# Two attention blocks on one core: the small matrix G transposed by a DMA on halves of its words instead of by TensorE, in six of eight images

## The chip, the cores and the metric

The kernel runs on one core of a Trainium2 chip. The metric is the device time of one launch, in microseconds (us). The core has five instruction streams that run beside each other and meet only at semaphores: TensorE (PE; its weight loads are listed as PEld), VectorE (DVE), ScalarE (ACT), GpSimd (POOL) and SyncE (SP), which here only issues DMAs. Each stream takes its instructions in the order written, so an instruction that waits holds up everything behind it on its stream, the DMA queue of SyncE included.

## The reference

The input x has 8 images of 512 channels and 64 x 64 pixels. Two layers follow each other.

```python
# layer 0
f = conv1x1(x, Wf, bf)                                  # 64 channels, 4096 pixels
g = maxpool2x2(conv1x1(x, Wg, bg)); v = maxpool2x2(conv1x1(x, Wh, bh))
beta = softmax(einsum('bcn,bcm->bnm', f, g), axis=-1)
o = einsum('bcm,bnm->bcn', v, beta)
x = gamma * conv1x1(o, Wv, bv) + x
# layer 1
Q = wq x + bq; K = wk x + bk; V = wv x + bv
Qf = delu(Q).transpose(0, 2, 1); Kf = delu(K)           # delu(x) = 10 relu(x) + exp(10 min(x, 0))
KV = einsum('bmn,bcn->bmc', Kf, V)
norm = 1 / einsum('bnd,bd->bn', Qf, sum(Kf, -1) + EPS)
out = x + gamma * einsum('bnd,bdc,bn->bcn', Qf, KV, norm)
```

All is in 32-bit floats. Layer 1 is linear in V, so the kernel does not form V. It sums G = Kf x^T (64 x 512) over an image and then multiplies by wv once: KV = G wv^T plus a term of the bias. That product needs G with its 512 channels on the partitions, hence a transposed G.

## The kernel before

An image is cut into 8 chunks of 512 pixels, 64 chunks in all. The program is a loop over steps s; one step works on several chunks at different stages at once. Layer 0's exponentials E of chunk s+1 are made and summed while the products M of chunk s (values by normalised E, in seven block products after Winograd and Strassen) and its projection N back to 512 channels run. The last chunk's layer 1 features are used in the same step, and f, g and v of chunk a = s + 9 are formed. Each piece is registered with a number, `at(t, fn)`, and the pieces of a step are issued in the order of t. So t is a place in an order written by hand, not a time, and it holds on all five streams.

The first step of an image (j == 0) closes the image before it, b_c. Step 8 is the first such step. These pieces of it matter, with t and line:

- `gather(s-1)` at 12.6 and 13.5: the last product pg (L727) and its addition to G (L736, VectorE). G is a tile of 128 x 512: rows 0 to 63 hold the sum of even blocks of pixels, rows 64 to 127 that of odd ones.
- `normalize` at 12.65, 13.7 and 38.6: the divisors pd of layer 1 (L818), their reciprocal rq_pd on VectorE (L825), its way to DRAM (L827, tile rn_row) and back, spread over the partitions (L831, two DMAs, tile rn), and at 38.6 the product qq (L837). The reciprocal lies in a tile of tag "rq", which has one buffer.
- `total` and `invert` of chunk s+1 at 17.85 and 18.0: the sum of E over the keys (L464) and its reciprocal on VectorE (L474), into a tile of the same tag "rq".
- `spread_inverses` at 18.01: this reciprocal to DRAM (L479, tile rd) and back on all partitions (L481, tile rb). `keep_inverses` at 23.0: ScalarE copies it to PSUM (L485, tile rtot). `normalize_block` multiplies the quarters of E by it (L499, VectorE, from 24.3 on).
- `bias_v` at 18.5, `split_v` at 18.6 and `turn_v` at 18.7: bias and transposition of v (L359 and L366 on ScalarE, L371 on SyncE); `join_v` at 32.0.
- `turn_G` at 21.2: four matmuls with the matrix `two` (L774), whose product is the transposed G with its two halves of rows added, and a copy scaled by gamma to the tile gT (L778, ScalarE).
- `project` at 24.8 and after: N in seven products; the first is copied out by ScalarE (L596, twice for one pair of blocks), added to x by GpSimd (L599), and its bank is then used on by the fourth product. Further additions are on VectorE (L602, L607).
- `features` at 35.0 (L633), and `features_exp` and so on.
- `make_KV` in the next step, at 5.5: pkv from gT and the weights (L791), after the first three M products and before the exponentials' products s (L407) of that step.

Words are transposed elsewhere in the kernel by a DMA that can turn 16-bit elements: ScalarE splits 32-bit words into high and low halves (`split_x` L682, 128 x 1024 halves), SyncE issues a transposing DMA (`turn_halves` L688), and a copy joins the halves (`join_x` L695 on ScalarE, `join_k` L674 on GpSimd with half as many). Chunks of x use the tiles w0 to w3 and u0 to u3 for that, one buffer each; the splits of a step stand at 33.8 to 36.8.

Scratch tiles come from a pool of seven buffers of 128 x 512 words, in turn; PSUM's eight banks are given out in turn as well.

Of the kernel before, what the change touches and what calls it, by code (L numbers as in the profile page):

```python
# [36 lines left out]
F32 = mybir.dt.float32  # L37
U16 = mybir.dt.uint16
AF = mybir.ActivationFunctionType
ALU = mybir.AluOpType  # L40
# [4 lines left out]
P = 128  # L45
QP = 32
CH = 512
# [4 lines left out]
def tile_two_attention_blocks(  # L52
# [21 lines left out]
    nc = tc.nc  # L74
    B, C, H, W = x.shape
    N = H * W
    D = WfT.shape[1]
    CV = WhT.shape[1]
    KT = C // P
# [5 lines left out]
    TOTAL = B * NCHUNK  # L85
# [24 lines left out]
    g1 = const.tile([P, 1], F32, name="g1")  # L110
# [69 lines left out]
    def run(ctx, general):  # L180
# [6 lines left out]
        work1 = ctx.enter_context(tc.tile_pool(name="work1", bufs=1))  # L187
# [7 lines left out]
        def bank(name):  # L195
            return psum.tile([P, CH], F32, tag="m", name=name)

        def scratch(name):
            return temp.tile([P, CH], F32, tag="t", name=name)
# [39 lines left out]
        st = {}  # L239
# [479 lines left out]
        def gather(s, at, t, t_out):  # L719

            b, j = divmod(s, NCHUNK)
            G, m = st[b]["G"], {}

            def product():
                pg = m["pg"] = bank(f"pg_{s}")
                for t in range(NT):
                    nc.tensor.matmul(  # L727
                        pg[half(t % 2), :], kTs[s][:, t, :], xTs[s][:, t, :],
                        start=(t < 2), stop=(t >= NT - 2),
                    )  # L730

            def out():
                if j == 0:
                    nc.vector.tensor_copy(G, m["pg"])
                else:
                    nc.vector.tensor_tensor(G, G, m["pg"], ALU.add)  # L736

            at(t, product)
            at(t_out, out)
# [24 lines left out]
                    kb[half(e), half(e)], ones[half(e), 0:D], ksum[half(e)], EPS, ALU.mult, ALU.add  # L764
                )

        def turn_G(b, at, t):

            s = st[b]

            def product():
                pt = bank(f"pGT_{b}").rearrange("p (k d) -> p k d", d=P)[:, :, 0:D]
                for k in range(KT):
                    nc.tensor.matmul(  # L774
                        pt[:, k, :], s["G"][:, bass.ts(k, P)], two, start=True, stop=True
                    )
                gT = s["gT"] = work1.tile([P, KT, D], F32, tag="gT", name=f"gT_{b}")
                nc.scalar.mul(gT, pt, g1)  # L778

            at(t, product)  # L780

        def make_KV(b, at, t, t_out):

            s = st[b]
            hc = C // 2

            def product():
                pkv = s["pkv"] = bank(f"pkv_{b}")
                for k in range(KT):
                    for h in range(2):  # L790
                        nc.tensor.matmul(  # L791
                            pkv[half(h), 0:hc], s["gT"][:, k, :], s["w_v1"][:, k, bass.ts(h, hc)],
                            start=(k == 0), stop=(k == KT - 1),
                        )

            def out():
                kv = s["kv"] = work1.tile([P, C], F32, tag="kv", name=f"kv_{b}")
                for h in range(2):
                    c = bass.ts(h, hc)
                    nc.vector.scalar_tensor_tensor(  # L800
                        kv[half(h), c], b_v1[half(h), c], s["ksum"][half(h)], s["pkv"][half(h), 0:hc],
                        ALU.mult, ALU.add,
                    )
                nc.gpsimd.tensor_copy(kv[half(1), 0:hc], kv[half(0), 0:hc])
                nc.vector.tensor_copy(kv[half(0), hc:C], kv[half(1), hc:C])

            at(t, product)
            at(t_out, out)
# [147 lines left out]
        def step(s):  # L956
            here, after = 0 <= s < TOTAL, 0 <= s + 1 < TOTAL
            a = s + LEAD
            b, j = divmod(s, NCHUNK)
            b_c = b - 1  # L960
# [4 lines left out]
            def at(t, fn, *args):  # L965
                work.append((t, len(work), fn, args))
# [45 lines left out]
                    gather(s - 1, at, *((30.9, 32.6) if late_k else (12.6, 13.5)))  # L1012
            if c_here and here and j == 0:
                at(0.2, start_kb, b_c)
                turn_G(b_c, at, 21.2 if a < TOTAL else 19.5)
                if a >= TOTAL:
                    make_KV(b_c, at, 21.4, 24.2)
            if s == TOTAL - NCHUNK:
# [32 lines left out]
            if after:  # L1051
                n = s + 1
# [6 lines left out]
                if not here:  # L1059
                    t, t_invert = 24.85, 24.86  # L1060
                elif s == 0 or a == TOTAL:
                    t, t_invert = 21.2, 22.6
                elif a > TOTAL and s % 2 == 0:
                    t, t_invert = 19.55, 19.6
                else:
                    t, t_invert = 16.1 if j % 2 == 1 and c_here else 17.85, 18.0
# [47 lines left out]
            if s == TOTAL:  # L1114
                pairs = [first // 2 + i for i in range(NCHUNK // 2)]
                x_last[s - 1] = [x_b[s - 1][:, k, :] for k in range(KT)]
                stored[s - 1] = [(x_b[s - 1], 0, KT)]
                at(-0.45, copy_x, s - 1)
                at(0.1, turn_k, s - 1)
                at(0.2, start_kb, B - 1)  # L1120
                gather(s - 1, at, 0.25, 0.35)
                at(0.4, divisors, pairs[0])
                turn_G(B - 1, at, 0.5)
                at(0.6, divisors, pairs[1])
                at(0.7, invert_divisors, 0)
                make_KV(B - 1, at, 0.9, 1.2)
                at(1.0, spread, pairs[0])
                at(1.1, divisors, pairs[2])
                at(1.15, spread, pairs[1])
                at(1.25, divisors, pairs[3])  # L1130
                at(1.3, scale, pairs[0])
                at(1.4, scale, pairs[1])
                at(1.6, invert_divisors, 1)
                for i, p in enumerate(pairs):
                    for k in range(KT):
                        at(7.0 + 4 * i + k, finish_last, p, k)
                    if i < 2:
                        at(8.6 + i, spread, pairs[i + 2])
                        at(10.5 + i, scale, pairs[i + 2])
                    for h in range(2):  # L1140
                        at(8.5 + 4 * i + 2 * h, store_last, p, h)
# [6 lines left out]
        for s in range(-LEAD, TOTAL + 1):  # L1148
            step(s)
# [5 lines left out]
    with ExitStack() as stack, tc.manual_schedule(engines=ENGINES):  # L1155
        run(stack, general=False)
# [12 lines left out]
    with tc.If(again > 0):  # L1169
        with ExitStack() as stack, tc.manual_schedule(engines=ENGINES):  # L1170
            run(stack, general=True)
# [37 lines left out]
```

## Time and profile before

| | us |
|---|---|
| median of 3 runs | 2599.88 (2599.7 to 2600.54) |
| the profiled execution | 2600.86 |
| its span, first to last instruction | 2599.0 |
| TensorE busy | 2561.7 |
| VectorE busy | 1957.4 |
| ScalarE busy | 1587.6 |
| GpSimd busy | 772.0 |

The profile is of one execution. A group of its page is one line of the kernel with one form of instruction: busy time in all, mean length in ns, idle time of the engine just before them and what ended most of it. The chain of waits follows the end of the program back from instruction to what released it. The timeline lists instructions in order of time, in us from the start of the span. A 32-bit matmul is recorded as two passes, each with its weight load. For a DMA the record is that of its issue on the queue.

### The profile page before, as it was taken

Reading aid. Unit: us, or ns where it says so; the run is one execution under the profiler, and the core shown is the slowest. Engines: PE = TensorE matmul, PEld = TensorE weight load, DVE = VectorE, ACT = ScalarE, POOL = GpSimd, SP = SyncE. Lnnn points to the kernel's source line nnn. Section 1 sums busy time; section 2 is a strip of 40 time slices with the busy share of each in tenths; the row PEclk is TensorE's granted clock in tenths of the full one; section 3 lists DMA queues with packets and bytes.
Section 4 is the critical chain, followed back from the end, with each engine's and each line's share of the span. In section 5 each row is a group of like instructions: output and inputs, shape, how many; then the busy total and the mean of one; then the engine's idle time right before and its main releaser. Section 6 shows DMA issues by size and latency. Waiting matters only on the chain.

```text
span 2599.0 us, 32002 instructions
## 1 busy us (share of the span) xinstructions
PE 2561.7 (99%) x11207; PEld 1765.2 (68%) x11207; DVE 1957.4 (75%) x3000; ACT 1587.6 (61%) x2724; POOL 772.0 (30%) x618
## 2 busy tenths in 40 slices
PE   8999999999999999999999999999999999999997
PEld 6667767667667667676676676666676666766664
DVE  5777778777777777777777777777777777788884
ACT  3375566566665675665665665666755656656662
POOL 4422323322323324223233223332233232221112
PEclk9999999999999999999999999999999999999999
DMA  5154455576565675565755566755657655665658
GB/s 171 55 136 100 130 146 141 135 177 138 148 168 132 167 175 123 160 158 135 178 143 156 150 137 161 188 130 148 164 131 183 142 149 146 146 144 141 160 142 278
DMA packets 488730, 390.68 MB, mean 150 GB/s; under 512 B 342072, under 2 KB 357360, under 8 KB 488560
## 3 DMA queue, kind: packets, MB, share of 16 engines
q1 hardware_dynamic: 471312, 329.03, 46.1%
q0 software_dynamic: 15232, 58.72, 12.3%
q8 instruction: 91, 1.49, 0.2%
q10 hardware_dynamic: 2016, 0.79, 0.1%
q14 instruction: 79, 0.65, 0.1%
HBM read 173.41 MB, written 133.39 MB: 118 GB/s over the span
## 4 chain that ended last, share of the span: by engine, by line
PE 90%; DVE 3%; DMA 1%; issue 1%; ACT 0%; POOL 0%; DVEq 0%; ACTq 0%; SPq 0%
PE M L523 29%; PE N L586 14%; PE H L316 12%; PE s L407 8%; PE pk L633 8%; PE fg L272 7%; PE pg L727 4%; PE pa L855 4%; PE tot L464 1%; PE pa L934 1%; DVE E L499 1%; PE pkv L791 1%; DMA xb<-in_x_dram 0%; PE pd L818 0%; DMA rb<-rd 0%
## 5 line engine op out<-in xcount | busy, mean ns | idle before, releaser
L599 POOL TENSOR_TENSOR xb<-xb,n 128x512 f32<-128x512 f32 x192 | 245.2, 1277 | 470.7 <-ACT n L596 460.2
L523 PE MATMUL M<-T,S 128*128 128x256 f32 x1536 | 364.5, 388 | 0.0
L499 DVE TENSOR_TENSOR E<-E,rtot 128x1024 f32<-128x1024 f32 x256 | 307.4, 1223 | 70.8 <-ACT rtot L485 68.9
L523 PEld LDWEIGHTS M<-T,S 128*128 128x128 f32 x1536 | 282.8, 190 | 81.1 <-ACT E L411 24.9
L695 ACT COPY xT<-u 128x1024 uint16<-128x1024 uint16 x252 | 328.3, 1353 | 1.4
L682 ACT COPY w<-xb 128x1024 uint16<-128x1024 uint16 x252 | 244.8, 1042 | 88.0 <-DVE xb L602 88.0
L596 ACT ACTIVATE n<-N,gb_v 128x256 f32<-128x256 f32 x384 | 161.1, 471 | 215.3 <-PE N L586 215.3
L411 ACT ACTIVATE E<-s 128x512 f32<-128x512 f32 x512 | 256.9, 619 | 33.4 <-DVE T L514 18.9
L674 POOL COPY kT<-uk 128x512 uint16<-128x512 uint16 x56 | 67.1, 1198 | 621.3 <-DMA uk<-wk 621.3
L586 PE MATMUL N<-to,w_v 128*128 128x256 f32 x1024 | 243.8, 380 | 3.8 <-ACT n L596 3.6
L407 PE MATMUL s<-f,g 64*128 64x512 f32 x1024 | 240.0, 604 | 2.8 <-DVE o L532 2.8
L523 PE MATMUL M<-E,vT 128*128 128x256 f32 x1024 | 231.8, 379 | 2.1 <-DVE E L499 2.1
L633 PE MATMUL pk<-xb,w_kqk 128*128 128x512 f32 x512 | 230.5, 593 | 1.9 <-DVE xb L607 1.9
L305 POOL TENSOR_TENSOR tha<-xa 128x512 f32<-128x512 f32 x59 | 80.6, 1366 | 499.1 <-PE M L523 462.2
L586 PEld LDWEIGHTS N<-to,w_v 128*128 128x128 f32 x1024 | 193.2, 190 | 33.9 <-ACT n L596 6.9
L602 DVE TENSOR_TENSOR xb<-xb,N 128x512 f32<-128x512 f32 x256 | 173.6, 683 | 55.5 <-POOL xb L599 53.3
L523 PEld LDWEIGHTS M<-E,vT 128*128 128x128 f32 x1024 | 194.4, 190 | 29.7 <-issue 3.4
L272 PE MATMUL fg<-xa,w_fg 128*128 128x512 f32 x472 | 212.5, 593 | 0.0
L445 DVE TENSOR_TENSOR r<-E 128x1024 f32<-128x1024 f32 x64 | 78.4, 1225 | 166.5 <-ACT E L411 166.5
L586 PE MATMUL N<-o,w_v 128*128 128x256 f32 x768 | 188.4, 381 | 1.7 <-ACT n L596 0.9
L586 PEld LDWEIGHTS N<-o,w_v 128*128 128x128 f32 x768 | 144.6, 190 | 56.5 <-issue 35.7
L485 ACT COPY rtot<-rb 128x512 f32<-128x512 f32 x54 | 31.8, 589 | 240.9 <-DMA rb<-rd 240.9
(160 smaller groups left out, 4516.1 us busy)
## 6 DMA issues: line engine op xcount, KB each, us to landing
xb<-in_x_dram SPq DMA_DIRECT2D x64, 1024.0 KB
out_dram<-xb SPq DMA_DIRECT2D x63, 1024.0 KB
xa<-in_x_dram SPq DMA_DIRECT2D x59, 1024.0 KB
out_dram<-y POOLq DMA_DIRECT2D x56, 1024.0 KB, 10.6
rb<-rd SPq DMA_DIRECT2D x54, 256.0 KB
w_v<-in_L_conv_wv_dram SPq DMA_DIRECT2D x8, 1024.0 KB
rn<-rn_row SPq DMA_DIRECT2D x56, 128.0 KB
x_early<-in_x_dram SPq DMA_DIRECT2D x4, 1024.0 KB
```

Of the source, the lines that this page charges most:

```text
L272: nc.tensor.matmul(fg, w_fg[:, k, :], x_a[a][:, k, :], start=(k == 0), stop=(k == KT - 1))
L316: nc.tensor.matmul(m[i], w_h7[i][:, k, :], th[a][i][:, k, :], start=(k == 0), stop=(k == hk - 1))
L407: nc.tensor.matmul(sc[e], g[half(e), i, :], fs[s][half(e), :], start=True, stop=True)
L411: nc.scalar.activation(es[s][:, 2 * i + e, :], sc[e], AF.Exp)
L499: nc.vector.tensor_tensor(b, b, r, ALU.mult)
L523: nc.tensor.matmul(m[i], v7[i][:, k, :], te[s][i][:, k, :], start=(k == 0), stop=(k == hm - 1))
L586: nc.tensor.matmul(a[:, k, :], w_v7[i][:, bass.ts(k, P)], b, start=not more and k == 0, stop=True, skip_group_check=more or k > 0,)
L599: nc.gpsimd.tensor_tensor(of_x(*ij), of_x(*ij), u, ALU.add)
L602: nc.vector.tensor_tensor(of_x(*ij), of_x(*ij), m[i], op)
L633: nc.tensor.matmul(pk, w_kqk[:, i, e * D : (e + 2) * D], x_b[s][:, i, :], start=(i == 0), stop=(i == KT - 1),)
L682: nc.scalar.copy(w, x_b[s][:, k, :].bitcast(U16).rearrange("p (n h) -> p h n", h=2))
L695: nc.scalar.copy(v[:, k], u)
```

## The change

In the six images that are closed while a chunk is still being prepared (`a < TOTAL`, steps 8, 16, 24, 32, 40 and 48), G is split into high and low halves by ScalarE (128 x 1024 halves), turned by a DMA from SyncE, joined by GpSimd into a scratch tile g2, and VectorE adds its two halves and scales the sum by gamma. The four stand at 13.6, 13.65, 22.5 and 38.7 of the same step. The old form, under the name `turn_G_now`, stays in the last two images.

```diff
-        def turn_G(b, at, t):
+        def turn_G_now(b, at, t):
...
+        def turn_G(b, at, ts):
+
+            s = st[b]
+            w = work1.tile([P, 2, CH], U16, tag="w3", name=f"wG_{b}")
+            u = work1.tile([P, 2 * KT, P], U16, tag="u3", name=f"uG_{b}")
+            g2 = scratch(f"g2_{b}").rearrange("p (k i) -> p k i", k=KT)
+
+            def split():
+                nc.scalar.copy(w, s["G"].bitcast(U16).rearrange("p (n h) -> p h n", h=2))
+
+            def turn():
+                nc.sync.dma_start_transpose(out=u, in_=w.rearrange("p h n -> p (h n)"))
+
+            def join():
+                nc.gpsimd.tensor_copy(
+                    g2.bitcast(U16).rearrange("p k (i h) -> p h k i", h=2),
+                    u.rearrange("p (h k) i -> p h k i", h=2),
+                )
+
+            def out():
+                gT = s["gT"] = work1.tile([P, KT, D], F32, tag="gT", name=f"gT_{b}")
+                nc.vector.scalar_tensor_tensor(
+                    gT, g2[:, :, 0:D], 1.0, g2[:, :, D:P], ALU.mult, ALU.add
+                )
+                nc.vector.tensor_scalar(gT, gT, g1, None, ALU.mult)
+
+            for t, fn in zip(ts, (split, turn, join, out)):
+                at(t, fn)
...
-                turn_G(b_c, at, 21.2 if a < TOTAL else 19.5)
+                if a < TOTAL:
+                    turn_G(b_c, at, (13.6, 13.65, 22.5, 38.7))
+                else:
+                    turn_G_now(b_c, at, 19.5)
...
-                turn_G(B - 1, at, 0.5)
+                turn_G_now(B - 1, at, 0.5)
```

## The prediction

> **What bounds the kernel now.** I read the page first, then the chain of waits, then the timeline of one affected step, then the waits. On the page TensorE is busy nearly all the time and the chain that ended last is 90% TensorE:
>
> ```profile
> PE 2561.7 (99%) x11207; PEld 1765.2 (68%) x11207; DVE 1957.4 (75%) x3000; ACT 1587.6 (61%) x2724; POOL 772.0 (30%) x618
> PE 90%; DVE 3%; DMA 1%; issue 1%; ACT 0%; POOL 0%; DVEq 0%; ACTq 0%; SPq 0%
> ```
>
> So work taken off TensorE could pay. The chain of waits prices the removed work, in step 8 (first image turned):
>
> ```profile
> 421.04 3.65 PE M L523 x16
> 424.69 0.84 PE pGT L774 x8
> 425.53 3.49 PE fg L272 x8
> 429.02 4.57 PE N L586 x20
> ```
>
> pGT holds the chain for 0.84 us; the change drops it for six images, 6 x 0.84 = 5.0 us at most. But twenty passes of N at 0.214 us are 4.28, and the chain gives 4.57: 0.29 us of waiting is inside. The timeline of the same step (start, length, engine, line; in brackets the idle time before and its releaser) says for what:
>
> ```profile
> 419.60 0.68 DVE L736 TENSOR_TENSOR G<-G,pg 128x512 f32<-128x512 f32 x1
> 420.19 0.95 DVE L825 RECIPROCAL rq_pd<-pd 128x128 f32<-128x128 f32 x1
> 421.17 0.60 SPq L827 DMA_DIRECT2D rn_row<-rq_pd  x1
> 423.52 1.32 SPq L831 DMA_DIRECT2D rn<-rn_row  x2
> 423.59 0.96 DVE L474 RECIPROCAL rq<-tot 128x128 f32<-128x128 f32 x1 [2.17 <-DMA rn_row<-rq_pd]
> 424.94 0.56 SPq L479 DMA_DIRECT2D rd<-rq  x1
> 425.57 0.47 ACT L778 ACTIVATE gT<-pGT,g 128x256 f32<-128x256 f32 x1 [7.36 <-PE pGT L774]
> 426.97 0.35 SPq L481 DMA_DIRECT2D rb<-rd  x1
> 430.19 0.59 ACT L485 COPY rtot<-rb 128x512 f32<-128x512 f32 x1 [3.43 <-DMA rb<-rd]
> 430.71 0.83 ACT L596 ACTIVATE n<-N,gb_v 128x256 f32<-128x256 f32 x2
> 431.60 1.59 PEld L586 LDWEIGHTS N<-to,w_v 128*128 128x128 f32 x8 [0.39 <-ACT n L596]
> ```
>
> Read it as one chain: the reciprocal rq_pd goes to DRAM (L827); the next reciprocal, L474, uses the same single buffer rq and waits until that transfer has read it (2.17 us idle); its result goes out and back (L479, L481), ScalarE copies it (L485), only then copies the first N out (L596), and TensorE's thirteenth pass of N waits for that. **This chain through SyncE's queue ends last in the step**, not pGT. From pGT's first weight load (424.32) the L596 pair ends at 7.23, 7.43, 7.28, 6.84, 6.80 and 8.48 us in the six images (same stretch of the timeline in each), and TensorE starts that pass at 7.28, 7.48, 7.33, 7.13, 7.13, 8.53. It waits in four of six; in two the chain has 0.24 and 0.28 us to spare.
>
> **What the Trainium skill says.** "VectorE: DVE Perf Modes", The three transpose paths: a 128x128 transpose in bf16 costs 390 ns on TensorE and 1309 by the DMA crossbar. The trace agrees in the direction: four blocks of G cost 0.84 us of TensorE, a transposing transfer of 128x1024 words 1.28 us of queue alone. "Perfetto Trace Analysis", Summary: the profiler window per engine type: for a DMA issued by SyncE the record is its issue, the data movement is hidden. Here uk's record lasts 1.20 us (407.90), yet GpSimd got the data at 410.57, 2.67 us after the start. "DMA: Bandwidth & Descriptors", HWDGE ordering: each DMA engine takes descriptors in ring order. The trace fits: rn_row took 2.35 us from issue to release while the three 1 MB loads ahead of it held the engines until 422.0 (DMA share 1.00 from 409.85 to 422.00), and 1.72 in images three and five.
>
> **The change, part by part.** 24 matmuls (48 passes) and six gT copies go. Each of six images gets four steps.
>
> 1. Split, ScalarE, at 13.6, after L736 and before bias_v. G is final at 420.28; L682, the same copy (128x1024 words), has mean 1042 ns. So 420.3 to 421.36. ScalarE is idle there (7.36 us), so it costs nothing by itself; behind it L359 and L366 (0.75 + 0.62) move from 416.8 to 421.4, ending at 422.7. Their customer, turn_v's transfer, goes out at 427.41: hidden.
> 2. Turn, SyncE, at 13.65, ahead of L827 at 13.7. **This is the step that costs.** It waits for the split, starts at 421.42 (a start within 0.06 to 0.08 of the copy's end, as at 400.62 after the copy of 399.50), and u's transfers, the same size, hold the queue 1.28 us (median of 252). So L827 starts at 422.76 in place of 421.17: 1.59 later. Queued behind it on SyncE are L831 (two), L479, L481 and turn_v; L474 waits for its landing. The landing: before, 2.35, 2.04, 1.72, 2.11, 1.72, 1.75 us after the issue, mean 1.95; later the loads are done, so 1.72, plus what the transfer's own packets keep it. The trace has no such pair: 0 if they are through, 0.5 if it queues behind them. In the DMA packets of the trace those of u end about 2.5 us after its issue and those of rn_row start 1.1 after its own, 1.35 + 1.1 after the turn, so they just clear; I take 0.15. The delay d = 1.59 + 1.87 - 1.95 = 1.5 us, and every link after it (L474, L479, L481, L485, L596) moves by d.
> 3. Join, GpSimd, at 22.5, behind L308 (ends 425.54). L674 copies half as many words in 0.76 to 1.71 us, so 1.5 to 3.4; the data is there by 424.2. It ends by 429.0; the next user of GpSimd, L599, starts at 431.6 + d. Hidden. The vector chain beside it (L544 to L556, ends 427.95 + d) may be slowed; N1, N2 and N4 must end only by 431.6 + d, so over 2 us are spare.
> 4. Out, VectorE, at 38.7: an addition of 128x256 words (L544: 0.42 to 0.51) and a scaling (between L280's 0.29 for a quarter of them and 0.42). About 0.8 us behind L837, which ends at 448.19; VectorE is full there, so L511, L514 and L532 move by 0.8. Customers: pkv at 450.09 wants gT (ready 449.0, 1.1 spare), the first exp of the next step at 453.13 wants L514 (450.47 + 0.8, 1.8 spare); both move with d as well. Hidden. Without that cover 0.8 per image is the bound.
>
> Buffers: w3 and u3 are free (their x halves were used at -0.45) and wanted again by the split of x near 440; the new scratch tile's slot is next written a whole step later; no bank or scratch wait falls on the chain. Extra traffic is 1.5 MB in 391.
>
> The sum. TensorE now reaches the pass 0.84 earlier and waits: it starts d later than before where it waited, d - 0.24 and d - 0.28 where it did not. From there to pk (the features' products, 439.65) it has 0.2 us of slack, and VectorE, whose E multiplications start from the same rtot, is busy without a gap from 430.81 to 439.87; so the shift is kept. 6 x 1.5 - 0.52 = +8.5 us. Against the profiled execution (2600.86, span 2599.0) that is 2609.4; its time stands 0.98 above the median of the runs, so the median goes from 2599.88 to **2608.4**. A measurement can tell about 0.2% here, 5.2 us: d must exceed 0.95.
>
> **The rivals.**
> A, the above: +6 to +12 (x from 0 to 0.5 gives 7.6 to 10.6; image variation the rest). For it: every link is a wait that the trace names.
> B, more: rn_row waits for the whole transposing transfer (2.67 as for uk, instead of 1.35), d = 2.8, or VectorE's 0.8 loses its cover in each image as well: +13 to +17. Against it: uk's neighbour out_dram goes out 0.06 us after uk's issue ends.
> C, no change: the queue issues the turn without holding L827, or the chain has hidden slack. With d = 0 TensorE's gain turns into waiting in four images and 0.5 us is left in all: -0.5. For it: nothing but that pairing being unseen.
> D, the other side: the L596 wait follows TensorE, not the queue, so that pGT's time comes out whole: -5.0, 2594.9. It decides at d below 0. Against it: L485's idle time names the DMA rb in all six. Even D is just under 0.2%, so faster needs D and luck.
> E, the change doesn't do what it says: the built order of instructions shows the 24 matmuls gone and the four steps in the places named, so I give it nothing.
>
> **How the numbers follow.** A 0.70, B 0.14, C 0.13, D 0.03. Slower by over 0.2%: A less its lowest edge, and B, 0.83; within: C, most of D and A's edge, 0.15; faster 0.02. The range takes A whole, leaves room below for a d near 0.6 and above for most of B: 2602.5 to 2615.
>
> **What would show it.** Right: L827 and L474 about 1.5 us later against L736, L485 named with the DMA rb, TensorE idle before that N pass near 2.6 us in each of six steps, pGT gone, gT's two vector operations beside no new TensorE wait. Wrong: L827 at its old distance from L736; or TensorE waiting at pkv or the s products for VectorE; or the stall recovered before pk.

## The result and the profile after

The changed kernel takes 2619.47 us (median of 6 runs, 2616.41 to 2621.52) against 2600.21 before: a ratio of 1.0072, 95% interval 1.0062 to 1.0082. It is 19.3 us slower where 8.5 were forecast, and outside the range given. The profiled execution took 2621.52, its span 2619.6: 20.7 us more than the profiled one of before.

The page after, its line of the engines and the chain that ended last, by engine:

```profile
PE 2565.6 (98%) x11159; PEld 1765.6 (67%) x11159; DVE 1960.4 (75%) x3012; ACT 1590.9 (61%) x2724; POOL 779.3 (30%) x624
...
PE 84%; DVE 7%; DMA 2%; ACT 2%; issue 1%; POOL 0%; SPq 0%; DVEq 0%; ACTq 0%
```

Forty-eight passes fewer, and yet TensorE is busy 3.9 us longer: some passes must have become slower. And its share of the chain fell from 90% to 84%: VectorE, DMA and ScalarE now lie on it. Where the time went shows when each step's pk (the features' products) is set against the same pk of before. In steps 1 to 7 the distance between the two traces does not change, nor does it by more than 0.1 us in any step after 8 other than the six that were changed. In those six it grows by 4.12, 3.86, 3.26, 2.26, 3.93 and 3.18 us, 20.6 in all, which is the whole difference.

The timeline of step 8, the same chain as shown for before (start, length, engine, line, idle time before and its releaser):

```profile
418.25 0.68 DVE L736 TENSOR_TENSOR G<-G,pg 128x512 f32<-128x512 f32 x1
...
419.03 1.04 ACT L790 COPY wG<-G 128x1024 uint16<-128x1024 uint16 x1 [3.37 <-DVE G L736]
...
420.10 2.48 SPq L793 DMA_TRANSPOSE uG<-wG  x1
...
422.68 0.59 SPq L856 DMA_DIRECT2D rn_row<-rq_pd  x1
...
424.41 1.32 SPq L860 DMA_DIRECT2D rn<-rn_row  x2
424.45 0.96 DVE L474 RECIPROCAL rq<-tot 128x128 f32<-128x128 f32 x1 [4.37 <-DMA rn_row<-rq_pd]
...
425.78 0.55 SPq L479 DMA_DIRECT2D rd<-rq  x1
...
428.13 0.36 SPq L481 DMA_DIRECT2D rb<-rd  x1
...
431.57 0.59 ACT L485 COPY rtot<-rb 128x512 f32<-128x512 f32 x1 [5.32 <-DMA rb<-rd]
432.10 0.83 ACT L596 ACTIVATE n<-N,gb_v 128x256 f32<-128x256 f32 x2
...
432.98 3.58 PE L586 MATMUL N<-to,w_v 128*128 128x256 f32 x8 [3.07 <-ACT n L596]
```

The numbers of the lines after the change are higher: L856 is the old L827, L860 the old L831. Read it downwards. G ends at 418.94. The transposing transfer holds SyncE's queue from 420.10 to 422.58, so rn_row goes out 3.74 us after G's end in place of 0.89. VectorE's wait for it grew from 2.17 to 4.37 us, and everything behind it is late, down to the pass of N, which TensorE now waits 3.07 us for. So far this is the chain of the prediction. The new thing is the last line: eight passes take 3.58 us, where in the kernel before twelve took 3.01:

```profile
430.58 3.01 PE L586 MATMUL N<-to,w_v 128*128 128x256 f32 x12
```

The stretches of that time after the change, with the granted clock in the third column from the end, say why:

```profile
428.00:432.80 4.80, 1.91 (x8) 1.19 (x8) 1.33 (x4) 1.23 (x3) 0.00 (x0) 1.00 0.40 82
432.80:436.20 3.40, 3.22 (x8) 2.57 (x9) 3.32 (x5) 1.24 (x4) 1.46 (x2) 0.50 0.00 0
436.20:440.00 3.80, 3.80 (x19) 3.36 (x18) 3.64 (x5) 2.65 (x6) 1.85 (x2) 1.00 0.00 0
```

For 3.4 us right after the stall TensorE's clock was granted at half. The stall does not only cost its own length; it makes the work that comes next slow. That happened in five of the six steps, all but the fourth: from the start of that pass to pk TensorE needs 9.46 to 9.56 us in these five and 7.99 in the fourth, so the half clock costs some 1.5 us each time.

### The profile page after: what moved, and what is told of

It reads as the page before. It is cut to its first block, busy times and chain, and to the rows that moved or that the text cites. A ratio compares the mean times of both kernels' runs of the same rounds, so it can differ in the third digit from the quotient of the medians.

```text
span 2619.6 us, 31948 instructions
## 1 busy us (share of the span) xinstructions
PE 2565.6 (98%) x11159; PEld 1765.6 (67%) x11159; DVE 1960.4 (75%) x3012; ACT 1590.9 (61%) x2724; POOL 779.3 (30%) x624
## 4 chain that ended last, share of the span: by engine, by line
PE 84%; DVE 7%; DMA 2%; ACT 2%; issue 1%; POOL 0%; SPq 0%; DVEq 0%; ACTq 0%
PE M L523 27%; PE N L586 13%; PE H L316 12%; PE s L407 8%; PE pk L633 8%; PE fg L272 6%; PE pg L727 4%; PE pa L884 4%; DVE E L499 1%; DMA rb<-rd 1%; DVE r L447 1%; PE tot L464 1%; ACT E L411 1%; PE pa L963 1%; PE pkv L820 1%
## 5 line engine op out<-in xcount | busy, mean ns | idle before, releaser
L596 ACT ACTIVATE n<-N,gb_v 128x256 f32<-128x256 f32 x384 | 160.8, 470 | 222.5 <-PE N L586 222.5
L586 PE MATMUL N<-to,w_v 128*128 128x256 f32 x1024 | 252.2, 389 | 19.7 <-ACT n L596 19.6
```

The lines of the kernel that those rows point to most:

```text
L586: nc.tensor.matmul(a[:, k, :], w_v7[i][:, bass.ts(k, P)], b, start=not more and k == 0, stop=True, skip_group_check=more or k > 0,)
```

## The experiments

Two theories stood at first. **The queue and the clock**: the place of the transposing transfer on SyncE's queue delays the chain rn_row, L474, rd, rb, rtot, L596; TensorE's stall on it costs its length, and lets the clock drop. **The steps themselves**: the wait of ScalarE for G, the join on GpSimd, VectorE's two operations or the extra traffic cost the time wherever the transfer stands. All times below stand against runs of the kernel before that share their chip: median 2601.31 for the first four, 2601.57 for the last four. A stall is the idle time of TensorE that the profile gives just before the pass of N that waits for L596.

**1. The transfer moved behind the chain.**

```diff
-                    turn_G(b_c, at, (13.6, 13.65, 22.5, 38.7))
+                    turn_G(b_c, at, (13.6, 18.75, 31.0, 38.7))
```

> All four steps of the change kept; only two places moved: the transposing transfer goes behind turn_v's (13.65 to 18.75), the join behind the last addition of n to x (22.5 to 31.0). Theory (the place on SyncE's queue is the whole cost: L827, L474, rd, rb, rtot late, then TensorE stalls about 3 us and its clock drops for one window): L827 and L474 back at their old distance from L736, no dropped clock, time 2599 to 2601. Rival (the steps cost by themselves: ScalarE waiting for G, the join on GpSimd, VectorE's two operations, the extra transfer): stays above 2608.

Measured: 2603.58, ratio 1.0005 (0.9997 to 1.0014), so no difference from the kernel before, and some 16 us less than the changed kernel with all four steps still there. SyncE's part of the timeline in step 8 (G ends at 419.09 here):

```profile
419.98 0.60 SPq L856 DMA_DIRECT2D rn_row<-rq_pd  x1
422.38 1.32 SPq L860 DMA_DIRECT2D rn<-rn_row  x2
...
427.57 1.30 SPq L793 DMA_TRANSPOSE uG<-wG  x1
```

rn_row is back at 0.89 us after G, and the transfer follows when nothing waits behind it. So the steps themselves are not the cause of the 19 us; the interval leaves them 3.6 at most. (The join was moved as well; in experiment 4 it stays at 22.5, and most of the time comes back there too.) The median lies above the expected 2599 to 2601 by 2.6; the kernel before itself stood 1.1 higher in these runs than in the first ones, and one step of the profile, the last of the six, still fell to half clock after a stall of 2.0 us; I had expected none to do so.

**2. The removed matmuls put back beside the new steps.**

```diff
-                gT = s["gT"] = work1.tile([P, KT, D], F32, tag="gT", name=f"gT_{b}")
+                gT = s["gT"]
...
                     turn_G(b_c, at, (13.6, 13.65, 22.5, 38.7))
+                    turn_G_now(b_c, at, 21.2)
```

> The changed kernel, with the removed pGT matmuls and their copy to gT put back at 21.2; the new steps stay, VectorE overwrites gT. TensorE has 0.84 us more work in each of the six steps. Theory (stall plus dropped clock): the chain to L596 does not move, so the pass of N starts where it did; the stall is 0.84 us shorter, so fewer windows drop to half clock, at about 1.7 us each: 2610 to 2619, not above the changed kernel. Rival (the extra 1.7 us after the stall has another cause, a bank or VectorE): the same 2619.5. Rival (TensorE's work counts): 2624.

Measured: 2620.64, ratio 1.0068 (1.0051 to 1.0085), the same as the changed kernel. So 0.84 us of TensorE's work in each of six steps cost nothing that can be measured, since TensorE only waits that much less; the 2624 of the last rival fell. But my own expectation was half a miss, 1.6 us above its range: I thought that with shorter stalls fewer windows would drop to half clock. The stalls were 2.02 to 2.21 us in five steps (3.45 in the sixth), and the clock dropped again in five steps of six; here a stretch of step 8:

```profile
433.00:436.00 3.00, 3.00 (x10) 2.35 (x9) 2.95 (x4) 2.08 (x4) 1.89 (x2) 0.53 0.00 0
```

The last section says why. The time alone would also fit the first rival (another cause of the slow passes), which forecast no change; experiment 7 decides about that one.

**3. The matmuls taken away and nothing put in their place.**

```diff
...
-                    turn_G(b_c, at, (13.6, 13.65, 22.5, 38.7))
+                    plain_G(b_c, at, 21.2)     # nc.scalar.mul(gT, first 256 columns of G, g1)
```

> pGT removed and none of the new steps put in its place: in the six images gT is a scaled copy of the first 256 columns of G as they stand, so KV is not the reference's there. It gives what the removal of pGT is worth alone. Theory (the chain through rn_row, rd, rb, rtot ends last, not TensorE): 0.5 us off the kernel before, 2599.7. Rival (TensorE bounds the step, the 0.84 us come out whole): 5.0 us off, 2595.

Measured: 2601.28, ratio 1.0003 (0.9994 to 1.0012). The rival's 5.0 us, a ratio of 0.998, lie outside the interval. Where TensorE is busy 99% of the time, 5 us of its work taken away gained nothing that can be measured: in every one of the six steps TensorE now waits for L596 (stalls of 0.44 to 1.86 us in this profile). In the second of them:

```profile
748.00 1.35 PE L586 MATMUL N<-to,w_v 128*128 128x256 f32 x5 [0.88 <-ACT n L596]
```

**4. The transfer in the hole of the queue**, between L827 and the two L831, where SyncE waits for rn_row anyway.

```diff
             at(t_invert, inversion)            # L825 and L827, 13.7
+            at(t_invert + 0.04, spread)        # the two L831
...
-                    turn_G(b_c, at, (13.6, 13.65, 22.5, 38.7))
+                    turn_G(b_c, at, (13.6, 13.72, 22.5, 38.7))
```

> The transposing transfer is issued between L827 (rn_row) and the two L831 (rn), where SyncE waits 1.7 to 2.4 us for rn_row to land; nothing else moved. Theory: L827 and L474 at their old distance from L736; rd late only where the issue of the turn takes longer than that wait (2.0 to 2.5 us in the first three images, 1.23 in the others): 2600 to 2605. Rival (the transfer's own packets hold rn_row or rb, wherever it is issued): 2610 or more.

Measured: 2605.26, ratio 1.0015 (1.0008 to 1.0022): 4.0 us slower, just above the upper edge of what was expected. rn_row goes out 0.90 us after G, as before. The issue of the transfer took 2.16, 1.83, 1.68, 1.26, 1.25 and 1.25 us, and L474 started 4.27, 3.82, 3.09, 2.68, 4.16 and 2.70 us after G: late in the steps where rn_row itself took long to land. That is not the transfer's doing alone: in experiment 3, without any transfer, L474 started 4.10 us after G in the fifth step too. One step fell to half clock.

**5 and 6. The chain that hid the matmuls taken apart**, with the change (transfer late as in 1) and without it. The edit of the chain is the same in both:

```diff
-                rd = work1.tile([P, P], F32, tag="rq", name=f"rq_pd_{pair}")
+                rd = work1.tile([P, P], F32, tag="rqd", name=f"rq_pd_{pair}")
...
             at(t_invert, inversion)
+            at(18.72, spread)                  # the two L831, behind turn_v's transfer
```

> The change with the transposing transfer late (18.75, join at 31.0), and the chain that ended last taken apart: rq_pd gets a buffer of its own, so L474 no longer waits for rn_row's landing, and the two rn DMAs go behind turn_v's transfer, so rd and rb go out earlier. Theory (that chain hid the removed matmuls): TensorE no longer waits for L596, pGT's 0.84 us come out in six images and the old waits with them, some 7 us off the kernel before: 2592 to 2596. Rival (rb is late for another reason, its transfer or the loads): within 2 us of the kernel before.

> The kernel before (pGT on TensorE in all images) with the same two edits of the chain and nothing of the change. Theory: only the old waits for L596 go (0.15, 0.35, 0.20, 0, 0 and 1.40 us), 2 us off, 2597 to 2599.5; so the kernel with the change and these edits should lie about 5 us below this one. Rival (the edits bring all): the same time as with the change.

Measured: with the change 2591.78, ratio 0.9962 (0.9948 to 0.9975); without it 2596.93, ratio 0.9984 (0.9977 to 0.9991). The two differ by 5.15 us and their runs do not overlap (at most 2593.0 against at least 2596.14): now, and only now, the removed 6 x 0.84 = 5.0 us come out. Both lie just below their ranges and gained some 2.5 us more than expected. In the profiles the six steps, where L596 no longer follows rtot at all, give 8.6 and 3.3 us for the 7 and 2 expected; the rest lies outside them, and I did not follow it. The timeline of the first of the two, step 8:

```profile
418.24 0.68 DVE L736 TENSOR_TENSOR G<-G,pg 128x512 f32<-128x512 f32 x1
...
419.82 0.60 SPq L856 DMA_DIRECT2D rn_row<-rq_pd  x1
419.98 0.94 DVE L474 RECIPROCAL rq<-tot 128x128 f32<-128x128 f32 x1
420.95 0.49 SPq L479 DMA_DIRECT2D rd<-rq  x1
...
422.60 0.34 SPq L481 DMA_DIRECT2D rb<-rd  x1
...
425.74 1.32 SPq L793 DMA_TRANSPOSE uG<-wG  x1
426.00 0.59 ACT L485 COPY rtot<-rb 128x512 f32<-128x512 f32 x1 [3.99 <-DMA rb<-rd]
...
426.63 1.89 PE L586 MATMUL N<-o,w_v 128*128 128x256 f32 x8
427.69 0.84 ACT L596 ACTIVATE n<-N,gb_v 128x256 f32<-128x256 f32 x2 [1.10 <-PE N L586]
```

L474 shows no wait for rn_row, rtot is there at 426.00, and L596 now waits for TensorE and no longer the other way round. This is the version that beats both kernels. The two edits of the chain were not tried apart. By the timelines the buffer gave most: L474 starts 1.06 us after G in five of the six steps (1.25 in the sixth) where it was 2.67 to 3.32 before, while rd follows the start of L474 by 0.97 us in place of about 1.35.

**7. The stall filled with work for nothing**, to test the clock.

```diff
+                pf = bank(f"fill_{b}")[:, 0:HN]
+                for i in range(5):
+                    nc.tensor.matmul(pf, ident, w_v[:, 0, 0:HN], start=True, stop=True)
...
+            at(26.6, fill)
```

> The changed kernel with five matmuls of 256 columns on the constant matrix ident added on TensorE behind N4, in the stall before the pass of N that waits (2.15 us of work for nothing in each of six steps, result unused). Theory (the stall drops the clock for one window of 3.4 us and that costs 1.7 us): no window at half clock in these steps, the pass starts where it did: about 8.5 us below the changed kernel, 2609 to 2613. Rival (the slow passes after the stall come from something else): 2619.5, or more by what the filling costs.

Measured: 2611.26, ratio 1.0040 (1.0026 to 1.0053), in the middle of what was expected and 8.2 us under the changed kernel: more work on the busiest engine made the kernel faster. Of this kernel the timeline of TensorE around the stall, and a stretch over it with the clock:

```profile
430.11 2.32 PE L811 MATMUL fill<-w_v,ident 128*128 128x256 f32 x10
433.17 1.99 PE L586 MATMUL N<-to,w_v 128*128 128x256 f32 x8 [0.73 <-ACT n L596]
```

```profile
431.00:435.00 4.00, 3.27 (x16) 2.56 (x14) 2.54 (x4) 2.02 (x5) 1.27 (x1) 1.00 0.13 22
```

The eight passes of N take 1.99 us where they took 3.58, and the clock stays at 1.00. None of the six steps dropped, and from that pass to pk TensorE needs 8.05 to 8.06 us in all six. The rival (another cause of the slow passes) is out. Not all of the gain is the clock's: between the two profiles the six steps are 9.2 us shorter, 7.3 of them after the start of the pass; 1.8 lie before it, since the pass started up to 0.9 us earlier against the pk ahead of it in five steps and 0.6 later in one. The filling does not explain that part.

**8. One load fewer ahead of the transfer**, to find what made the delay of L474 longer than I had it.

```diff
-                at(0.6, load_wv1, b_c)
+                at(30.0 if a < TOTAL else 0.6, load_wv1, b_c)
```

> The changed kernel with the 1 MB load of w_v1 moved from 0.6 to 30.0 in the six steps, so that two loads and not three stand ahead of the transposing transfer. Theory (the mis-sized part of the delay is the transfer and rn_row held up behind loads: the issue took 2.0 to 2.5 us in three images, rn_row's landing 2.0 to 2.5 in the others): the issue takes 1.2 to 1.3 in all, L474 is 1.2 to 1.6 us later than in the kernel before; with the clock still dropping 2613 to 2617, without 2607 to 2610. Rival (the delay is the transfer's own length): L474 stays 1.6 to 2.4 late, 2619.5.

Measured: 2616.38, ratio 1.0054 (1.0039 to 1.0070), as expected with the clock still dropping (it did in three steps). The records of the transfer's issue, minimum, median and maximum in ns, in the changed kernel and then in this one:

```profile
L793 SPq DMA_TRANSPOSE uG<-wG x6: 1232/1612/2480, 420.1 to 2021.8; - x6
```

```profile
L793 SPq DMA_TRANSPOSE uG<-wG x6: 1232/1232/2651, 421.5 to 2018.4; - x6
```

With the load gone the issue takes 1.23 to 1.39 us in five images. That alone does not show that the load was the reason: in experiments 2 and 7, with all three loads in place, it took 1.23 to 1.26 in five images of six as well. And the first image here took 2.65 us, the longest of all, though the DMA engines had stood still before it, from G's end to the start of the transfer (DMA share 0.00, the last column but one):

```profile
420.36:421.52 1.16, 1.16 (x12) 0.60 (x12) 1.14 (x2) 1.07 (x2) 1.08 (x2) 1.00 0.00 0
```

What the load does change is issue and landing together. In images two to six L474 started 4.44 to 4.50 us after G, against 4.51 to 5.45 in the same images of the changed kernel and of experiments 2 and 7, on average 0.4 us sooner. Set against the kernel before, L474 is later by 2.33, 1.46, 1.77, 1.41, 1.83 and 1.78 us, where the changed kernel has 2.20, 2.31, 2.36, 1.57, 2.39 and 1.84. Two of the six lie in the 1.2 to 1.6 that I expected and four in the rival's 1.6 to 2.4: the load ahead is a small part of the delay, and most of it stays without it.

## Why the prediction was wrong, point by point

- **What bounds the step.** Right. The chain through SyncE's queue, not TensorE, set the time (experiments 1, 3, 5 and 6), and it is why nothing of the 5.0 us came out.
- **Step 1, the split.** Right: 1.04 us, hidden.
- **Step 2, the turn.** The mechanism was right, its size wrong. The term mis-sized is the time that the transfer holds the queue: I took 1.28 us, the median of u's transfers, and it was 2.48, 2.28, 1.99, 1.23, 1.23 and 1.24, mean 1.74. The row that I took it from has a minimum of 1.23 and a maximum of 2.30, so the long case stood in it. The landing of rn_row, 1.87 in my sum, was 1.73, 1.72, 1.71, 2.08, 2.53 and 1.96, mean 1.96. So d was 2.1 us and not 1.5. I had also put rn_row's slow landing in the first image of before (2.35 us) down to the loads. From 1 to 2 us after G the DMA share is 0.79 there, and 0.67 and 0.70 in images three and five, where it landed in 1.72: the loads end at nearly the same time, and explain little of that.
- **The start of the pass of N.** It moved by 2.72, 2.36, 1.75, 2.09, 2.14 and 1.68 us against the pk ahead of it, 12.7 in all in place of 8.5. Of the 4.2 between them, 3.7 come from d and 1.7 from G itself, which ended late against that pk by 0.41 in the fourth image and 1.30 in the sixth; I did not follow where those come from. Some 1.1 come back, mainly in the sixth image, where rtot came 5.0 us after rb's issue before the change and 3.2 after it.
- **"So the shift is kept"**, from that pass to pk. Wrong, and the largest miss: it grew by another 7.9 us, 1.4 to 1.8 in each of the five steps whose clock dropped and 0.2 in the fourth, whose clock did not. I had used the pass length of before for work that follows a stall that before does not have (its longest there is 1.24 us), and so put the clock at nothing. Experiment 7 shows the cause: with the stalls filled no step drops, and the stretch from that pass to pk is 7.3 us shorter in the six steps.
- **Steps 3 and 4.** Right: the join took 1.33 us and ended at 425.5, the addition and the scaling 0.42 and 0.35, and nobody waited for them.
- **The rivals.** B had the size (13 to 17) nearer than A, and was right in part. In the last three images, where the issue was short, rn_row landed 0.2 to 0.8 us later than the 1.72 of an idle queue; in the fifth its first packet moved 4.10 us after G, while those of the transfer ended at 4.22. But d was 2.1 and not 2.8, and VectorE kept its cover, so the size came near by luck: B has no clock in it. C's remainder of 0.5 us for d = 0 fits experiment 3, which cannot tell it from nothing. D fell.

The sum then: 12.7 at the pass of N, 7.9 by the clock, 20.6 in the six steps. The start and the end of the program differ by 1.3 in each direction between the two profiles and cancel; each has one stretch at half clock there that the other lacks (at 115 us before the change, at 2583 after it).

## What to carry to other kernels

A busy engine is not the bound of a stage while a chain of small transfers ends later in it: find what the engine waits for last, and take work off it only when that is gone. A DMA put ahead of another on a queue costs its issue there, and everything that follows in the queue; a median is a poor price for that where the issue of like transfers ranges from 1.2 to 2.5 us in one trace. And a stall of TensorE of some 2 us or more is to be priced at more than its length, since the passes after it may run at half clock; in this kernel work for nothing in the stall was cheaper than the stall.

## What the runs showed of the hardware that was not expected

**When the clock drops.** The clock record in the traces has stretches at half. Between matmuls most last 3.41 us, and two in experiment 8 twice that. Their starts and ends lie on a grid of 3.413 us through the whole trace, whose place differs from execution to execution. I counted how much of each window of this grid TensorE's matmul records fill, between 420 and 2060 us of ten traces (before, after and the eight experiments). In all 15 windows filled by 0.09 to 0.43 the next window was at half. In the four filled by 0.46 to 0.52, and in all that were fuller, it was not, with one exception: in experiment 8 a window filled by 0.81, itself at half, was followed by a second one.

Outside that range the count is less clean. Near the start and the end of the program windows filled by 0.44 to 0.46 went either way. And in three traces (after, experiments 2 and 5) a window near the end of the matmuls (2579.8 us after the change) was full by its records and yet followed by half clock; it holds mostly matmuls of 2 and 64 columns, so a full record may not be what counts. This stays open.

For the six steps it is the share of a fixed window that counts, not the length of a gap. In experiments 1, 2 and 4 stalls of 1.93 to 2.21 us brought the clock down in six steps, and stalls of 1.90 to 2.08 did not in four others, by their place on the grid; the stall of 2.83 us in the fourth step of the changed kernel fell on two windows, filled by 0.71 and 0.46, and did nothing. That is why experiment 2 missed. Whether it also makes the changed kernel's times spread by 5.1 us is not shown: only one execution of each kernel has a trace, and the kernel before, without such drops in its trace, spreads by 4.6 and 5.4 in the longer series. The Trainium skill, "TensorE: Matmul & The Clock Gate", What's actually happening, gives a free-running window of 3413 ns and two states, full and half; the length, the grid and the states agree with the traces. It names an idle window as what throttles; in these steps the traces put the point at a window less than about 0.45 filled.

**The length of a DMA's issue.** The same transposing transfer held SyncE's queue 1.23 us in three images and 1.99 to 2.48 in three others. Experiment 8 shows that the loads ahead are not the reason. The traces show something else that goes with it. The page lists a DMA queue named "instruction" with 91 packets; they are of 16 KB each. Of all 3752 issues of transposing transfers in the ten traces 217 took over 1.5 us, and during 216 of these such a packet was under way. Of the 3367 issues without one, a single one was that long; another 169 had one and stayed short. No run moved these packets, so they go with the long issues, but that they cause them is not shown.

**What the next DMA waits for.** In seven images of the changed kernel and of experiments 2 and 7 the issue was short, but the transfer's packets ran on until 3.88 to 4.63 us after G. The first packet of rn_row, which moves 3.73 us after G where the transfer is through by then, then came only 0.04 to 0.18 us before the transfer's last one ended. "DMA: Bandwidth & Descriptors" in the Trainium skill, HWDGE ordering, has each DMA engine consume the descriptors of its ring in order. That fits, but no run here shows the rings themselves.
